# Four edits to a four-layer graph network on one core: group sums, mask pieces, the last tiles' transposes, and the place of a layer's columns

## The chip, the cores and the metric

The kernel runs on one core of a Trainium2 chip. A core has five engines with a queue of their own each: TensorE (PE, matrix products; its weight loads are listed as PEld), VectorE (DVE), ScalarE (ACT), GpSimd (POOL) and SyncE (SP, which only issues DMAs here). SBUF is the working memory of 128 partitions, PSUM holds the results of PE in 8 banks per partition, and HBM is the main memory. Sixteen DMA engines move data between HBM and SBUF. The metric is the device time of one execution in microseconds; lower is better.

## The reference

Four layers run one after the other over 3327 nodes with 512 features and one adjacency matrix `adj` of 3327 x 3327. Each layer's result is added to its input and normalised by rows. Layers 0, 2 and 3 are attention over neighbours with 8, 8 and 4 heads; layer 1 takes the mean of the first 64 neighbours.

```python
def attention(h, adj, W, a):             # layers 0, 2 and 3
    Wh = h @ W                           # split into heads
    e = leaky_relu((Wh @ a1)[:, None] + (Wh @ a2)[None, :], 0.2)
    p = softmax(where(adj > 0, e, -9e15), axis=neighbours)
    return p @ Wh                        # per head; layers 2 and 3 put elu on it

def mean_layer(X, A):                    # layer 1
    keep = (A > 0) & (cumsum(A > 0, axis=1) <= 64)
    nb_mean = (keep @ X) / max(keep.sum(axis=1), 1)
    xj = leaky_relu(nb_mean @ W_nb.T + b_nb)
    return leaky_relu(X @ W_line.T + b_line) + where(keep.sum(axis=1) > 0, xj, 0)

x = layernorm(x + attention_0(x)); x = layernorm(x + mean_layer(x))
x = layernorm(x + attention_2(x)); x = layernorm(x + attention_3(x))
```

## The kernel before

The nodes are padded to 3328, that is 26 tiles of 128 (`NT`), in two halves of 13 tiles or 1664 columns (`HALF`, `IW`). A half is cut for PE into four column ranges of 448, 448, 384 and 384 (`CUTS`); the first two together are `WA` = 896 columns, the last two `WB` = 768.

**Attention of layers 0 and 2** (`unit8`, L659, called by `attention8`). Eight units run in order. Units 0 and 7 take two heads and one half of the columns each; units 1 to 6 take one head and all 3328 columns ("wide"). The units form four groups: unit 0; units 1 to 3; units 4 to 6; unit 7. A unit has 26 steps, one for each tile `j` of neighbours:

- DVE makes `t` (L695) from the row values `rb` of the head, a column value and the mask: one operation of 128x3328, or two of 128x1664. There are three `t` buffers. Layer 0 reads the mask from the SBUF array `mask0`, layer 2 from the tiles `mk`.
- ACT makes `y` from it (L696), which is needed for the denominators.
- PE multiplies `t` with the values `vj` into `po` (L717, 16 matmuls), then adds the denominators of the step before into two PSUM banks `pd` (L675: the function `den`). The first half of the columns lies in rows 0 to 63 of `pd` and fills 448 columns of each bank, the second in rows 64 to 127 and fills 384.

A job may be hung to each step: one from the list `background`, then one from the list `aside`. At the end of a unit ACT copies `po` to `ob` (L732); four transposes by PE and four stores of `hd` follow as background jobs of the next unit.

At the end of a group the denominators are read. ACT copies `pd` to `db` in four copies, two of 64x448 (L771) and two of 64x384 (L772). A background job `sums` on step 2 of the next unit multiplies them down with PE into `pe` (L780); the job `reciprocals` on step 4 makes `rec` of them with six DVE operations (L788 to L790). The last group takes another way.

**The mask of layer 0.** Its first half is made before the attention begins. The second half is made during units 0 and 1, as `aside` jobs: `mask_steps` (L873) yields a list of steps; step k has SP load piece k of the adjacency matrix into a buffer `raw`, and sets the mask from piece k - lag, on DVE (L870) or, for 4 of 9 pieces, on ACT (L869). A piece has 416 columns, so there are 104; three buffers, a lag of 2, and three steps hung to each step of the unit. From step 13 of unit 1 on PE counts the columns of that half of the mask (`count_jobs`, L889, matmuls at L900).

**Layer 1** (`sage`, L949) accumulates each of the 26 tiles with 52 matmuls (L1139). `output` (L1114) turns the sum into the tile `y`, stores it, and for all tiles but the last loads it again by four DMAs in blocks of 32x32 as `yx`. `job1` makes the transposed tile `xT` in `project1` (L259): by a DVE transpose from `yx` (L263), or from `y` with four PE transposes and an ACT copy (L267, L268). `job2` makes the projection for layer 2 from it (L277). Both are hung to steps of the next tiles' accumulation: `job1` of tile 24 at step 21 of tile 25, its `job2` behind it.

**Layer 3** (`third`, L1173) first finishes layer 2 tile by tile and projects each tile with the weights `wsb`, which POOL loads (L144), then runs an attention of its own. The arrays `sden` and `sm` are made in `piece_columns` (L251), where POOL sets them to zero; they lie in the pool `col3` with the layer's other columns, below `wsb` in memory. The space is that of layer 2's attention, whose pools start with a row buffer `rbb` (13,312 B per partition) and layer 2's own `sden`.

**What sets the order.** PE runs in the order in which the program is written (`manual_schedule`, L63). On the other engines a planner puts the instructions into an order ahead of time, by its own estimate of when each can start, the earlier written first among those that can; `keep_in_program_order` holds an instruction behind the one written before it on its engine. The engines then run that order strictly. The planner also derives every wait, those for memory that an earlier tile still uses among them.

Of the kernel before, what the change touches and what calls it, by code (L numbers as in the profile page):

```python
# [13 lines left out]
ALU = mybir.AluOpType  # L14
# [4 lines left out]
P = 128  # L19
# [13 lines left out]
def kernel(  # L33
# [10 lines left out]
    nc = tc.nc  # L44
    N, F = x.shape
    NT = (N + P - 1) // P
# [4 lines left out]
    HALF = NT // 2  # L51
    FW = F // 2
    assert F == 512 and NT % 2 == 0 and N < NP and NT < 32
    IW = HALF * P
    NA = (HALF + 1) // 2
    WA, WB = NA * P, IW - NA * P
# [41 lines left out]
    c1 = const.tile([P, 2, 16], F32, name="c1")  # L98
# [6 lines left out]
    for e in range(2):  # L105
        nc.vector.tensor_tensor(c1w[:, :, e, :], c1[:, :, 8 * e:8 * e + 4], c1[:, :, 8 * e + 4:8 * e + 8],
                                op=ALU.add)
# [551 lines left out]
    def unit8(self, pools, n, ring, background, aside, ending=None):  # L659
        tp, yp, vp, sp, po_p = pools  # L660
        u = UNITS[n]
# [3 lines left out]
        if u.first:  # L665
            self.pd = [po_p.tile([P, 512], F32, name=f"pd{c}") for c in range(2)]
            self.seen = set()
        pd, seen = self.pd, self.seen
        f0 = u.h * D
        FV = D if u.wide else 2 * D  # L670
# [91 lines left out]
        def by_head(a, k):  # L762
            t0 = u.base(k) // P
            return a[:, t0:t0 + HALF, :].rearrange("p t (s k) -> p t k s", k=2)[:, :, u.section(k), slots]

        db = sp.tile([P, WA], F32, name="db", bufs=1)
        if WB < WA:
            nc.gpsimd.memset(db[64:, WB:], 0.0)
        if not end:
            for c in range(2):  # L770
                nc.scalar.copy(db[:64, c * (WA // 2):(c + 1) * (WA // 2)], pd[c][:64, :WA // 2])  # L771
                nc.scalar.copy(db[64:, c * (WB // 2):(c + 1) * (WB // 2)], pd[c][64:, :WB // 2])  # L772
            held = []

            def sums():
                pe = qp.tile([P, HALF, 2, 2 * NS], F32, name="pe", tag="q")
                held.append(pe)
                for q in range(HALF):
                    e = int(q >= NA)
                    nc.tensor.matmul(pe[:, q, :, :], db[:, (q - e * NA) * P:(q - e * NA + 1) * P],  # L780
                                     c1[:, :, 8 * e:8 * e + 8], start=True, stop=True)

            def reciprocals():
                pv = held[0].rearrange("p t o (k s) -> p t o k s", k=2)
                for k in range(2):
                    r_ = by_head(rec, k)
                    tc.keep_in_program_order(
                        nc.vector.tensor_tensor(r_, pv[:, :, 0, k, slots], by_head(self.rc, k), op=ALU.mult))  # L788
                    nc.vector.tensor_tensor(r_, pv[:, :, 1, k, slots], r_, op=ALU.add)
                    nc.vector.reciprocal(r_, r_)  # L790

            return jobs[:2] + [sums, nothing, reciprocals] + jobs[2:]

        for c in range(2):
            ins = nc.vector.transpose(db[:64, c * (WA // 2):(c + 1) * (WA // 2)], pd[c][:64, :WA // 2])
# [153 lines left out]
    def sage(first, first_pool, xin, prev, nxt, wsrc, dst, ring):  # L949
# [5 lines left out]
        with tc.tile_pool(name="sg_z", bufs=1, reuse_waits="tile") as zp, \  # L955
# [138 lines left out]
            with tc.tile_pool(name="sb_w", bufs=1, reuse_waits="tile") as wp, \  # L1094
                    tc.tile_pool(name="sb_k", bufs=1, reuse_waits="tile") as kpb, \
                    tc.tile_pool(name="sb", bufs=1, reuse_waits="tile") as sp, \
                    tc.tile_pool(name="sb_ps", bufs=1, space=PSUM, reuse_waits="tile") as ps, \
                    tc.tile_pool(name="sb_pk", bufs=1, space=PSUM, reuse_waits="tile") as pkp:
                pools_k.append(kpb)
                wsb = wp.tile([P, FC, 2, FW + nxt.H], F32, name="wsb")  # L1100
                load_wide(wsb, wsrc, nc.sync)

                def bank(e):
                    return qp.tile([P, 512], F32, name="pw1", tag="q") if e else \
                        ps.tile([P, 512], F32, name="pw0")

                bnb = wp.tile([P, F], F32, name="bnb")
                nc.gpsimd.dma_start(out=bnb, in_=bn.to_broadcast([P, F]))

                seed(pkp, None)  # L1110
                carry_in(FIRST)
                carry_in(FIRST + 1)

                def output(acc, t):  # L1114
                    xi = sp.tile([P, F], F32, name="xi")
                    nc.gpsimd.dma_start(out=xi, in_=xid[t * P:(t + 1) * P, :])
                    y = sp.tile([P, F], F32, name="y", bufs=2)
                    nc.vector.scalar_tensor_tensor(y, acc, cnt[:, 1, t:t + 1], bnb, op0=ALU.mult, op1=ALU.add)
                    nc.vector.scalar_tensor_tensor(y, y, 0.01, y, op0=ALU.mult, op1=ALU.max)
                    nc.vector.scalar_tensor_tensor(y, y, cnt[:, 2, t:t + 1], xi, op0=ALU.mult, op1=ALU.add)  # L1120
                    norm_rows(sp, [y], t)
                    store_tile(dst, y, t, nc.sync)
                    if t == NT - 1:
                        return y

                    yx = sp.tile([P, FC, P], F32, name="yx")
                    for q in range(4):
                        nc.sync.dma_start(out=yx[32 * q:32 * q + 32].rearrange("p c (g f) -> p c g f", g=4),
                                          in_=dst[t * P:(t + 1) * P, :].rearrange("(g a) (c q f) -> q a c g f", g=4, q=4, f=32)[q])
                    return yx  # L1130

                jobs, side = [], []
                for b in range(len(blocks)):
                    t0, i0 = blocks[b]
                    for s in range(G):
                        acc = ps.tile([P, F], F32, name="acc", bufs=2)
                        for t in range(NT):
                            for c in range(2):
                                nc.tensor.matmul(acc, kts[b, t][:, s * P:(s + 1) * P], zs(t, c),  # L1139
                                                 start=t == 0 and c == 0, stop=t == NT - 1 and c == 1)  # L1140
                            if (s * NT + t) % 4 == 1:
                                kept()
                                carry_in(len(kts) // 2 + 1)

                            if jobs and (t == 9 and t0 + s > 1 or t == 21):
                                jobs.pop(0)()
                            if side and t == 14:
                                side.pop(0)()
                        if t0 + s == 0:
                            tc.keep_in_program_order(nc.vector.tensor_copy(  # L1150
                                wsb[:, :, :, FW:], wa[nxt.li].rearrange("p c (e h) -> p c e h", e=2)))
                        y = output(acc, t0 + s)
                        held = {}

                        def job1(y=y, t=t0 + s, held=held):
                            held["xT"] = nxt.project1(sp, ps, y, t, t < NT - 1)

                        def job2(t=t0 + s, held=held):
                            nxt.project2(sp, bank, wsb, held["xT"], t)
                            if t == HALF - 1:  # L1160
                                side.extend(nxt.prepare_steps(sp, 0, "xT", 1))

                        jobs += [job1, job2]
                    if b == len(blocks) - 2:
                        for j in range(mask_tiles.FIRST):
                            mask_tiles.load(j, 0, nc.gpsimd)
                        nxt.first_rows = nxt.wide_rows(ring, UNITS[0])
                while jobs:
                    jobs.pop(0)()
                nxt.mean(sp, bank, wsb)  # L1170


    def third(first):  # L1173
        with tc.tile_pool(name="col3", bufs=1) as cp:
            rp = mask_tiles.early.tile([P, 2, IW], F32, name="rba")
            L3.columns(cp)
            L3.more_columns(cp)
            L3.piece_columns(cp)
            with tc.tile_pool(name="p_w", bufs=1, reuse_waits="tile") as wp, \
                    tc.tile_pool(name="p", bufs=3, reuse_waits="tile") as pp, \  # L1180
                    tc.tile_pool(name="p_f", bufs=2, reuse_waits="tile") as fp, \
# [50 lines left out]
            with tc.tile_pool(name="f3", bufs=2) as fp, tc.tile_pool(name="f4", bufs=1) as gp:  # L1232
# [115 lines left out]
                for k, (q0, n, _, add1, add2) in enumerate(lasts):  # L1348
# [6 lines left out]
                    if k > 0:  # L1355
                        scale(*lasts[k - 1][:2])
                scale(*lasts[-1][:2])

    L0, L2, L3 = Layer(0, 8, False), Layer(2, 8, True), Layer(3, 4, True)

# [2 lines left out]
    with tc.tile_pool(name="mask0", bufs=1, reuse_waits="tile") as mp0, \  # L1363
# [84 lines left out]
            return []  # L1448


        pieces = [(t, q, IW // 4) for t in range(NT) for q in range(4, 8)]
        rest = ExitStack()
        rawp = rest.enter_context(tc.tile_pool(name="raw", bufs=3))
        ring.insert(0, (rest.enter_context(tc.tile_pool(name="at_s0", bufs=1, reuse_waits="tile")), "rbb"))
        msteps = mask_steps(rawp, pieces, 2, [k for k in range(len(pieces)) if k % 9 in (1, 3, 5, 7)], True)

        def some(n):
            for f in msteps[n:n + 3]:
                f()

        ends = []
        attention8(L0, ring, first_jobs, [lambda n=n: some(n) for n in range(0, len(msteps), 3)],
                     ending=lambda sp: ends.extend(finish(f0, x, L0, 0, 2, 2, nc.sync, None, sp)))
        rest.close()

# [75 lines left out]
```

## Time and profile before

| | us |
|---|---|
| median of 3 runs | 3266.63 |
| lowest and highest | 3264.71 and 3269.53 |
| profiled execution | 3265.22 |
| its span, from the first instruction to the last | 3263.5 |
| attention of layer 0, last `ob` copies of units 0 and 7 | 255.3 and 958.2 |
| last accumulation of layer 1 ends | 1604.3 |
| attention of layer 2, last `ob` copies of units 0 and 7 | 1746.3 and 2421.1 |

The costliest rows of the profile's table of groups that the text below uses (busy time and mean of one; behind the second bar the idle time just before them and what ended most of it):

```profile
L695 DVE SCALAR_TENSOR_TENSOR t<-rba,qc,mask 128x3328 f32<-128x3328 f32 x78 | 281.9, 3679 | 8.3 <-PE po L717 8.0
L870 DVE TENSOR_SCALAR mask<-raw 128x832 fp8e4<-128x832 int32 x50 | 30.2, 614 | 25.4 <-DMA raw<-in_adjT_dram 25.4
L870 DVE TENSOR_SCALAR mask<-raw 128x416 fp8e4<-128x416 int32 x43 | 15.4, 371 | 7.3 <-DMA raw<-in_adjT_dram 7.1
L771 ACT COPY db<-pd 64x448 f32<-64x448 f32 x12 | 6.3, 527 | 0.1
L772 ACT COPY db<-pd 64x384 f32<-64x384 f32 x12 | 5.7, 474 | 0.1
```

A row names the line of the kernel, the engine, the operation, the tile written and those read, the shapes and the number of instructions. The 832-column rows are those of the mask's first half, which is made before the attention.

### The profile page before, as it was taken

How to read it: one execution, taken by the hardware profiler on the slowest of the kernel's cores; microseconds unless marked ns; L12 is line 12 of the kernel's file. 1: busy time of each engine (PE TensorE's matmuls, PEld its weight loads, DVE VectorE, ACT ScalarE, POOL GpSimd, SP SyncE). 2: the span in 40 equal slices, each digit the busy share in tenths (PEclk: the TensorE clock that was granted, in tenths of full speed). 3: DMA queues.
4: the chain of work that ended last, by engine and by line, in shares of the span. 5: the costliest groups of instructions: out<-in, count | busy, mean ns of one | idle time of the engine just before them, and what ended most of it. 6: DMA issues, size and time to landing. Idle time of an engine off the chain costs nothing. (4 is left out here: it accounts for less than half of the span.)

```text
span 3263.5 us, 46836 instructions
## 1 busy us (share of the span) xinstructions
PE 3161.3 (97%) x18738; PEld 1598.6 (49%) x18738; DVE 2624.2 (80%) x2328; ACT 2299.9 (70%) x1859; POOL 235.4 (7%) x384
## 2 busy tenths in 40 slices
PE   8999999999999999999899999999998999999997
PEld 7643343333434467777634333333447654455443
DVE  5799999999977645555499999999988666677886
ACT  2598888899873334444388998899987555558976
POOL 3100000000010011111100000000011000010110
PEclk9999999999999999999999999999999999999998
DMA  9554114111134345555331111011137211122311
GB/s 364 179 171 139 42 53 153 40 42 41 29 105 124 101 132 136 142 131 152 97 124 55 41 35 39 20 42 41 32 113 237 80 42 43 42 52 88 94 39 50
DMA packets 364212, 300.47 MB, mean 92 GB/s; under 512 B 235394, under 2 KB 304456, under 8 KB 362459
## 3 DMA queue, kind: packets, MB, share of 16 engines
q1 hardware_dynamic: 331803, 186.19, 19.9%
q0 software_dynamic: 26672, 103.60, 10.3%
q10 hardware_dynamic: 5520, 7.69, 0.7%
q8 instruction: 148, 2.42, 0.3%
q14 instruction: 69, 0.57, 0.1%
HBM read 220.53 MB, written 76.84 MB: 91 GB/s over the span
## 5 line engine op out<-in xcount | busy, mean ns | idle before, releaser
L696 ACT ACTIVATE y<-t,bi,sc 128x3328 fp8e4<-128x3328 f32 (+1 forms) x520 | 1342.7, 2604 | 144.6 <-PE pd L675 91.2
L717 PE MATMUL po<-t,vj 128*64 128x448 f32 (+1 forms) x6656 | 1266.6, 522 | 15.4 <-DVE t L695 14.3
L717 PEld LDWEIGHTS po<-t,vj 128*64 128x64 f32 x6656 | 450.4, 137 | 699.4 <-issue 621.2
L451 PE MATMUL po<-t,vj 128*128 128x448 f32 (+1 forms) x1664 | 607.2, 518 | 1.4 <-DVE t L428 1.4
L428 DVE SCALAR_TENSOR_TENSOR t<-rba,qc,mk 128x1664 f32<-128x1664 f32 x208 | 404.1, 1949 | 163.8 <-PE po L451 145.9
L431 ACT ACTIVATE y<-t,bi,sc 128x1664 fp8e4<-128x1664 f32 x208 | 358.4, 1767 | 198.1 <-PE pd L403 190.3
L451 PEld LDWEIGHTS po<-t,vj 128*128 128x128 f32 x1664 | 307.8, 190 | 272.7 <-issue 181.0
L695 DVE SCALAR_TENSOR_TENSOR t<-rba,qc,mk 128x3328 f32<-128x3328 f32 (+1 forms) x130 | 379.8, 2987 | 11.2 <-DMA mk<-md 7.5
L695 DVE SCALAR_TENSOR_TENSOR t<-rba,qc,mask 128x3328 f32<-128x3328 f32 (+1 forms) x130 | 381.8, 2986 | 8.3 <-PE po L717 8.0
L695 DVE SCALAR_TENSOR_TENSOR t<-rbb,qc,mask 128x3328 f32<-128x3328 f32 (+1 forms) x130 | 381.5, 2985 | 6.6 <-PE po L717 4.1
L695 DVE SCALAR_TENSOR_TENSOR t<-rbb,qc,mk 128x3328 f32<-128x3328 f32 (+1 forms) x130 | 379.9, 2985 | 5.7 <-PE po L717 4.9
L1139 PE MATMUL acc<-zs,kt 128*128 128x512 f32 x1352 | 359.9, 420 | 0.0
L277 PE MATMUL pw<-wsb,xT 128*128 128x264 f32 (+1 forms) x1248 | 305.0, 400 | 17.7 <-ACT xT L268 5.1
L1139 PEld LDWEIGHTS acc<-zs,kt 128*128 128x128 f32 x1352 | 255.7, 189 | 52.2 <-PE pk L990 0.8
L277 PEld LDWEIGHTS pw<-wsb,xT 128*128 128x128 f32 x1248 | 243.5, 199 | 62.7 <-ACT xT L268 10.0
L997 ACT CAST pk<-cy 128x512 f32<-128x512 bf16 x169 | 99.1, 587 | 222.9 <-DVE kt L1011 216.4
L675 PE MATMUL pd<-y,sden 128*32 128x448 fp8e4 (+1 forms) x3328 | 241.3, 343 | 0.0
L1011 DVE SCALAR_TENSOR_TENSOR kt<-pk,mb 128x512 fp32r<-128x512 f32 x169 | 115.4, 684 | 116.6 <-PE pk L1008 115.4
L675 PEld LDWEIGHTS <-sden 128*32 128x32 bf16 x3328 | 86.7, 96 | 139.2 <-issue 119.6
L283 DVE TENSOR_TENSOR vt<-pw,dc 128x256 f32<-128x256 f32 x156 | 58.6, 417 | 96.5 <-ACT dc L278 90.5
L1037 PE MATMUL pz<-wn,xT 128*128 128x512 f32 x208 | 96.2, 606 | 6.2 <-DMA wn<-in_wnT_dram 5.9
L967 POOL DMA_DIRECT2D cy<-ctd x91 | 68.1, 748 | 366.3 <-ACT pk L997 297.1
(213 smaller groups left out, 2119.9 us busy)
## 6 DMA issues: line engine op xcount, KB each, us to landing
vj<-v SPq DMA_DIRECT2D x156, 128.0 KB
cy<-ctd POOLq DMA_DIRECT2D x78, 256.0 KB, 4.3
raw<-in_adjT_dram SPq DMA_DIRECT2D x42, 416.0 KB
h<-hd SPq DMA_DIRECT2D x61, 256.0 KB
raw<-in_adjT_dram SPq DMA_DIRECT2D x75, 208.0 KB
v<-vt SPq DMA_DIRECT2D x50, 256.0 KB
xr<-x POOLq DMA_DIRECT2D x45, 256.0 KB, 3.4
md<-mask SPq DMA_DIRECT2D x26, 416.0 KB
```

The source lines that it names most:

```text
L277: nc.tensor.matmul(pw[e][:, :FW + H], xT[:, c, :], wsb[:, c, e, :], start=c == 0, stop=c == FC - 1)
L428: nc.vector.scalar_tensor_tensor(t, rb[k], self.qc[:, j, h:h + 1], mask_at[0](j, i0, IW), op0=ALU.max, op1=ALU.mult)
L431: nc.scalar.activation(y, t, AF.Sigmoid, bias=self.bi[:, j, h:h + 1], scale=self.sc[:, j, h:h + 1], saturate=False)
L451: nc.tensor.matmul(po[c][k * D:(k + 1) * D, :z - a_], vj[:, j % 2, k * D:(k + 1) * D], ts[k][:, a_:z], start=j == 0, stop=j == NT - 1)
L675: nc.tensor.matmul(pd[c][32 * kk:32 * kk + 32, :w_], lhsT, rhs, start=(kk, c) not in seen, stop=last and j == NT - 1)
L695: nc.vector.scalar_tensor_tensor(to, ro, self.qc[:, j, h:h + 1], m, op0=ALU.max, op1=ALU.mult)
L696: nc.scalar.activation(yo, to, AF.Sigmoid, bias=self.bi[:, j, h:h + 1], scale=self.sc[:, j, h:h + 1], saturate=False)
L717: nc.tensor.matmul(po[c][k * D:(k + 1) * D, :z - a_], vj[:, j % 2, x_:x_ + D], t[:, k, a_:z], start=j == 0, stop=j == NT - 1)
L997: nc.scalar.copy(pks[k % 2], carry[b, t // 4 * 4][:, t % 4:t % 4 + 2, :])
L1011: nc.vector.scalar_tensor_tensor(kt, pk, NEIGHBOURS, mb[:, t:t + 2, :], op0=ALU.is_le, op1=ALU.mult)
L1037: nc.tensor.matmul(pz, xT[:, c, :], wn[:, c, :], start=c == 0, stop=c == FC - 1)
L1139: nc.tensor.matmul(acc, kts[b, t][:, s * P:(s + 1) * P], zs(t, c), start=t == 0 and c == 0, stop=t == NT - 1 and c == 1)
```

## The change

It has four parts.

1. **Group sums.** `pd` is copied in two copies of 128x448 instead of four. So that the 64 columns that the lower rows do not fill hold zeros, DVE sets them to zero when a group begins (groups 0, 1 and 2). POOL's zeroing of a part of `db` goes, but for the last group. `reciprocals` works on both heads or halves at once, in three DVE operations instead of six, and runs on step 6 of the unit instead of step 4; the first transpose job moves from step 5 to step 3.
2. **Mask pieces** of the second half have 832 columns instead of 416: 52 instead of 104, with two buffers instead of three and a lag of 1 instead of 2. A step of the unit takes one or two of them, four in three steps, so that they reach to step 13 of unit 1 instead of step 9.
3. **Layer 1's last two tiles**, not only the last, are transposed by PE.
4. **Layer 3's `sden` and `sm`** lie in a pool of their own at the other end of the memory.

```diff
@@ unit8
         if u.first:
             self.pd = [po_p.tile([P, 512], F32, name=f"pd{c}") for c in range(2)]
             self.seen = set()
+            if not u.half and WB < WA:
+                for c in range(2):
+                    nc.vector.memset(self.pd[c][64:, WB // 2:WA // 2], 0.0)
...
-        if WB < WA:
+        if end and WB < WA:
             nc.gpsimd.memset(db[64:, WB:], 0.0)
         if not end:
             for c in range(2):
-                nc.scalar.copy(db[:64, c * (WA // 2):(c + 1) * (WA // 2)], pd[c][:64, :WA // 2])
-                nc.scalar.copy(db[64:, c * (WB // 2):(c + 1) * (WB // 2)], pd[c][64:, :WB // 2])
+                nc.scalar.copy(db[:, c * (WA // 2):(c + 1) * (WA // 2)], pd[c][:, :WA // 2])
...
                 for q in range(HALF):
                     e = int(q >= NA)
-                    nc.tensor.matmul(pe[:, q, :, :], db[:, (q - e * NA) * P:(q - e * NA + 1) * P],
-                                     c1[:, :, 8 * e:8 * e + 8], start=True, stop=True)
+                    nb = WB // 2 // P
+                    x_ = q * P if not e else (q - NA) // nb * (WA // 2) + (q - NA) % nb * P
+                    nc.tensor.matmul(pe[:, q, :, :], db[:, x_:x_ + P], c1[:, :, 8 * e:8 * e + 8], start=True, stop=True)
 
             def reciprocals():
-                pv = held[0].rearrange("p t o (k s) -> p t o k s", k=2)
-                for k in range(2):
-                    r_ = by_head(rec, k)
-                    tc.keep_in_program_order(
-                        nc.vector.tensor_tensor(r_, pv[:, :, 0, k, slots], by_head(self.rc, k), op=ALU.mult))
-                    nc.vector.tensor_tensor(r_, pv[:, :, 1, k, slots], r_, op=ALU.add)
-                    nc.vector.reciprocal(r_, r_)
-
-            return jobs[:2] + [sums, nothing, reciprocals] + jobs[2:]
+                pv = held[0].rearrange("p t o (k s) -> p k t o s", k=2)
+
+                def both(a):
+                    if u.wide:
+                        return a.rearrange("p (k t) (s e) -> p k t s e", k=2, e=2)[:, :, :, slots, u.parity]
+                    return a[:, u.half * HALF:(u.half + 1) * HALF].rearrange("p t (s k) -> p k t s", k=2)[:, :, :, slots]
+
+                r_ = both(rec)
+                tc.keep_in_program_order(
+                    nc.vector.tensor_tensor(r_, pv[:, :, :, 0, slots], both(self.rc), op=ALU.mult))
+                nc.vector.tensor_tensor(r_, pv[:, :, :, 1, slots], r_, op=ALU.add)
+                nc.vector.reciprocal(r_, r_)
+
+            return jobs[:2] + [sums] + jobs[2:4] + [nothing, reciprocals] + jobs[4:]
@@ sage
-                    if t == NT - 1:
+                    if t >= NT - 2:
                         return y
...
-                            held["xT"] = nxt.project1(sp, ps, y, t, t < NT - 1)
+                            held["xT"] = nxt.project1(sp, ps, y, t, t < NT - 2)
@@ third
-            L3.piece_columns(cp)
+            sums = ExitStack()
+            L3.piece_columns(sums.enter_context(tc.tile_pool(name="more3", bufs=1, side="right")))
...
+                sums.close()
@@ layer 0
-        pieces = [(t, q, IW // 4) for t in range(NT) for q in range(4, 8)]
+        pieces = [(t, q, IW // 2) for t in range(NT) for q in range(2, 4)]
         rest = ExitStack()
-        rawp = rest.enter_context(tc.tile_pool(name="raw", bufs=3))
+        rawp = rest.enter_context(tc.tile_pool(name="raw", bufs=2))
...
-        msteps = mask_steps(rawp, pieces, 2, [k for k in range(len(pieces)) if k % 9 in (1, 3, 5, 7)], True)
+        msteps = mask_steps(rawp, pieces, 1, [k for k in range(len(pieces)) if k % 9 in (1, 3, 5, 7)], True)
 
         def some(n):
-            for f in msteps[n:n + 3]:
+            for f in msteps[4 * n // 3:4 * (n + 1) // 3]:
                 f()
...
-        attention8(L0, ring, first_jobs, [lambda n=n: some(n) for n in range(0, len(msteps), 3)],
+        attention8(L0, ring, first_jobs, [lambda n=n: some(n) for n in range(len(msteps) * 3 // 4 + 1)],
```

## The prediction

> **What bounds the kernel now.** I read the page's busy table first, then TensorE's gaps in time, then for each gap the timeline of the engine it waited for.
>
> ```profile
> PE 3161.3 (97%) x18738; PEld 1598.6 (49%) x18738; DVE 2624.2 (80%) x2328; ACT 2299.9 (70%) x1859; POOL 235.4 (7%) x384
> ```
>
> PE is busy for 97% of the span, so an edit pays only where PE stands idle, or runs slowly after standing idle. Such places are few, and the four parts of the change lie at some of them. Between two ends of `ob` copies in the attention of layers 0 and 2, a unit that starts no group lasts some 94.5 us and PE is busy through all of it (unit 2 of layer 2: 94.5 of 94.5, windows of the trace), DVE for 93.8. What DVE or ACT saves there is worth nothing; what makes PE wait is lost in full.
>
> The timeline of DVE where unit 0 of layer 0 ends (start, duration, instruction; in brackets the idle time ahead and what ended it):
>
> ```profile
> 250.77 3.68 DVE L695 SCALAR_TENSOR_TENSOR t<-rbb,qc,mask 128x3328 f32<-128x3328 f32 x1
> 254.37 0.37 DVE L870 TENSOR_SCALAR mask<-raw 128x415 fp8e4<-128x415 int32 x1
> 259.01 0.38 DVE L870 TENSOR_SCALAR mask<-raw 128x416 fp8e4<-128x416 int32 x1 [4.27 <-DMA raw<-in_adjT_dram]
> 259.30 3.68 DVE L695 SCALAR_TENSOR_TENSOR t<-rbb,qc,mask 128x3328 f32<-128x3328 f32 x1
> ```
>
> DVE waits 4.27 us for a mask piece, in order, with the next product behind it; PE then starts 3.18 us late at 263.04. From 246 to 314 us PE loses 1.67 + 3.18 + 0.68 + 0.26 + 0.31 + 0.87 + 0.12 + 0.38 = 7.47 us to DVE (my list of PE gaps over 0.1 us).
>
> PE at the end of layer 1:
>
> ```profile
> 1596.53 7.81 PE L1139 MATMUL acc<-zs,kt 128*128 128x512 f32 x32
> 1607.41 6.83 PE L277 MATMUL pw<-wsb,xT 128*128 128x264 f32 x16 [3.07 <-DVE xT L263]
> 1614.77 0.66 PE L267 MATMUL pt<-ident,y 128*128 128x128 f32 x4 [0.53 <-ACT y L162]
> ```
>
> Tile 24's `xT` is late: its DVE transpose stood behind three operations of tile 25. The 16 matmuls after the gap take 6.83 us; the same 16 at 1593.16 took 3.72.
>
> POOL, then PE, at the start of layer 3:
>
> ```profile
> 2414.25 2.01 POOL L254 MEMSET sden<- 128x2288 bf16 x1 [42.69 <-DVE t L695]
> 2420.64 0.54 POOL L127 DMA_DIRECT2D xr<-x  x1 [3.17 <-ACT h L162]
> 2422.23 1.52 POOL L144 DMA_DIRECT2D wsb<-in_w_dram  x2
> ```
>
> ```profile
> 2429.00 0.89 PE L277 MATMUL pw<-wsb,xT 128*128 128x260 f32 x2 [4.02 <-DMA wsb<-in_w_dram]
> ```
>
> The weights are issued at 2422.23, and PE waits 4.02 us for them. From 2420 to 2440 the 16 DMA engines are 0.73 to 1.07 busy, before 2420 at most 0.15 (windows).
>
> ACT, then PE, where unit 1 of layer 2 begins:
>
> ```profile
> 1749.72 0.52 ACT L771 COPY db<-pd 64x448 f32<-64x448 f32 x1
> ...
> 1751.30 0.47 ACT L772 COPY db<-pd 64x384 f32<-64x384 f32 x1
> ```
>
> ```profile
> 1751.38 0.81 PE L675 MATMUL pd<-mk,sm 128*32 128x448 fp8e4 x8
> ```
>
> The copies end just as the next group's first sums in the same `pd` start.
>
> **What the Trainium skill says.** "DMA: Bandwidth & Descriptors", "Queues, rings and completion order": a DMA engine takes turns between queues packet by packet. The trace agrees: at 250.87 POOL issues the rows of unit 2, whose packets are 13,312 B and take 498 ns; a mask packet (1,664 B) takes 69. The piece issued at 250.88 needs 6.4 us to its last packet, the median of 100 pieces is 2.3. "TensorE: Matmul & The Clock Gate", part 1: after an idle window of about 3.4 us PE drops to half clock. The trace agrees (6.83 against 3.72 us, after a shorter gap of 3.07; clock 0.50 in 2430 to 2435). "PSUM — Partial Sum Buffer", "PSUM bank collisions raise a hardware error": different engines must be kept apart by bank and quadrant, not by address. So I take it that the new memset is ordered against copies and sums of its bank; no trace here shows it yet.
>
> **Group sums: +2.5 us.** Each of six group ends has two 64-row copies less: ACT 2 x (526 + 474) becomes 2 x 526 ns, 0.95 us saved, off the path. The divisions become 3 DVE operations from 6: by the rows (117 and 160, 172 and 195, 232 and 393 ns for 13 and 39 columns) I extend to 26 or 78 columns: about 0.4 us saved a group, 2.4 in all. The 12 new DVE memsets of 64x64 take it back: an estimate of 0.15 us each from the smallest DVE rows, 1.8. The later read gains nothing: DVE waited 0.5 us in all for `pe`. The POOL memset that goes held up only row loads whose buffers were not free. What counts is the new chain copies, memset, first sums. DVE is strictly in order and its slots are one product apart, 3.61 us in unit 1 of layer 2: 1749.07, then 1752.68. With half the copies done at 1750.8, the memsets fall at 1752.7, end at 1753.0, and PE waits 1.6 us. In the groups at 565 and 2032 us copies end at 566.9 and 2034.0, slots at 568.2 and 2035.3 precede the sums (570.6, 2037.6): nothing. At 255 us I take 0.9 of a possible wait of 1, since DVE's slot 266.8 follows the 265.98 of the sums. Bounds: 0, where the planner always finds an earlier slot, and +8.5 where each misses one (3 x 1.6 + 3.7).
>
> **Mask pieces: -5.5 us.** A set of 416 columns takes 371 ns (0.28 from start to start), of 832 columns 614: I take 0.53. The 5 of 9 pieces on DVE: 58 x 0.28 = 16.2 becomes 29 x 0.53 = 15.4. Four thirds of a piece per step instead of three small ones move work out of unit 0: there 43 x 0.28 = 12.1 becomes 19 x 0.53 = 10.1, so DVE reaches unit 1 about 2 us earlier, plus its small waits for pieces in unit 0 (0.34 + 0.37 + 1.08 + 0.13 + 0.22 + 0.09 = 2.2 us) where they vanish, with three `t` buffers as lead. In unit 1 a step costs DVE 3.60 + 0.39 = 3.99 for 14 steps instead of 4.07 for 10. Two pieces in flight hold 1,664 columns instead of 1,248, 1.5 steps instead of one, and beside the row load a piece of the same 128 packets brings twice the columns. SP issues half as many loads. I take 5.5 of the 7.47 us; bounds 0 (the stall at 255 merely moves) and -7.5.
>
> **Tile 24 by PE: -3.5 us.** Its four transposes (0.66, the row above) go into tile 25's accumulation at step 21, near 1602.4; `y` is ready since 1595.7, ACT is idle, so `xT` is there by 1603.8. The accumulation ends at 1605.0 instead of 1604.34, the projection follows at once at full clock: 1608.7 instead of 1614.24. Tile 25 then waits for its own chain: three DVE operations 2.2, statistics 0.75, table and root 1.6, DVE 0.6, ACT 0.8: `y` at 1611.1, where it now ends at 1614.7. SP loses four reloads, DVE one transpose. From there all shifts by 3.5. Bounds -1.5, if ACT loads its exponential table ahead of the root (1.28 more), and -4.5.
>
> **Layer 3's columns: -4 us.** By the pool sizes in the code, `wsb` (8,320 B per partition) lay at bytes 8,320 to 16,640 of the space that layer 2's attention leaves, over the row buffer (13,312 B) and layer 2's `sden`, read until PE's last sums at 2421.4. With 6,240 B gone from below it, it lies in the row buffer alone, free at 2414.1 when DVE has read it last. So POOL can issue it there; the memset ahead of it moves away. One MB passes in the idle 2414 to 2420. That takes it out of the crowd: `h<-hd`, for which DVE waits 4.18 us until 2436.49, should land near 2432.5, and the chain of `h` that starts PE at 2440.95 with it. PE's own waits for `wsb` (4.02 + 0.54 us) lie beside that chain and are not added. The memset waits under the other stack's `hb` and `red` until their stores land, estimate 2428 to 2431 from the 2425.26 issue of `dd`; behind it stand loads of `xr` that are used after 2454. Bounds -5.5, and 0 if POOL's order stays.
>
> **Sum.** +2.5 - 5.5 - 3.5 - 4 = -10.5. The profiled execution took 3265.22 (span 3263.5 and 1.7 around it), which gives 3254.7; the median of the runs is 1.4 above it: 3256 us.
>
> **Rivals.** (1) Partial: the piece in flight is caught by the row load anyway, or `wsb` is issued where it was. Without the mask gain -5.0, 3261.6; without layer 3's -6.5, 3260.1. For it: the row load is unchanged. Against it: more columns in flight. (2) The other side, slower: PE counts mask columns at step 13 of unit 1 in fixed order (L900, 317.49), and the piece before that is now planned for step 12, formerly 9. Sets run behind their steps: the last one, of step 9, ran after the product of step 13, at 313.75. If they still lag four to five steps, PE waits 3.7 us for each step beyond two: 4 such steps give +15 - 10.5 = +4.5, 3271. It decides from a lag of five steps on. Against it: 43,264 columns took 174 us with three small buffers; two large ones, at 2.8 + 2 to 3 us a turn (estimate: median 2.3, plus 0.5 for the bytes, plus a slot), are about a tenth faster. (3) The memset misses its slot everywhere: +6, so -4.5, 3262. (4) POOL's moved memset is put ahead of `wsb`: issue near 2431 + 2.8, PE 9 us later: about +3 in all, 3269.
>
> **How the numbers follow.** Less than 0.2% (6.5 us) cannot be told from no change. My forecast has 0.48, rival 1 0.24, 2 0.12, 3 0.10, 4 0.06. Faster takes the forecast and half of rival 1: 0.60; slower, half of 2, part of 4 and what I have not thought of: 0.12; same the rest, 0.28. Bounds summed give 3249 below (all at their best, -17.5) and 3272 above; I close at 3270. The forecast alone: 3249 to 3260.
>
> **What would show it.** Right: no PE gap of 3 us near 260; 16 projection matmuls in 3.7 us after layer 1's last accumulation; `wsb` issued by POOL near 2415, none of PE's 4 us. Wrong: PE waiting for DVE's `pd` memset by more than 2 us at 255, 565, 1744 and 2030; L900 in unit 1 waiting for a mask set; the POOL memset ahead of the weights.

## The result and the profile after

The changed kernel took 3257.87 us (median of 11 runs, 3252.65 to 3261.62), the kernel before beside it 3264.71 us. The ratio is 0.9976, with 95% interval 0.9967 to 0.9986: 7.8 us faster, between 4.6 and 10.8. A second series beside other kernels gave 0.9979 (0.9972 to 0.9986). The profiled execution took 3255.54 us with a span of 3253.8, 9.7 us less than the one of before. The time forecast was 3256, from a sum of -10.5 us on the profiled execution of before; the measured interval holds a gain of that size.

The busy line of the page hardly moves, as it should: the work is the same, and only TensorE's idle time and clock can change.

```profile
PE 3160.6 (97%) x18742; PEld 1603.0 (49%) x18742; DVE 2622.6 (81%) x2292; ACT 2290.4 (70%) x1827; POOL 233.7 (7%) x378
```

To see where the time went I took instructions that stand in both traces in the same place of the program and compared their start times. The shift, after minus before, is +1.3 us ahead of layer 0's attention (the loads at the start vary by that much between executions), -1.3 after unit 1 of layer 0, -0.7 in layer 1, -3.2 after its end, -1.9 after unit 1 of layer 2, -8.6 from the first products of layer 3 on, and -8.8 at the last matmuls; the other 0.9 us of the span lie behind them. So the gain arises in layer 0, at the end of layer 1 and at the start of layer 3, and the start of unit 1 in layer 2 gives some back. Each is read below, with the lines that answer to those shown of before. Line numbers are those of each run's own kernel, so L698 here is L695 of before.

DVE where unit 0 of layer 0 ends:

```profile
249.78 0.60 DVE L878 TENSOR_SCALAR mask<-raw 128x831 fp8e4<-128x831 int32 x1
250.28 3.69 DVE L698 SCALAR_TENSOR_TENSOR t<-rbb,qc,mask 128x3328 f32<-128x3328 f32 x1
258.32 0.60 DVE L878 TENSOR_SCALAR mask<-raw 128x831 fp8e4<-128x831 int32 x1 [4.35 <-DMA raw<-in_adjT_dram]
258.83 7.27 DVE L698 SCALAR_TENSOR_TENSOR t<-rbb,qc,mask 128x3328 f32<-128x3328 f32 x2
```

```profile
262.56 4.71 PE L720 MATMUL po<-t,vj 128*64 128x448 f32 x16 [2.97 <-DVE t L698]
```

The wait for the mask piece that I expected to go is there, 4.35 us where it was 4.27, and PE's gap behind it is 2.97 us where it was 3.18. The row load is issued at 250.17 and this piece at 250.41. What layer 0 gains comes from smaller waits, which are read with the experiments.

PE at the end of layer 1:

```profile
1604.01 3.72 PE L277 MATMUL pw<-wsb,xT 128*128 128x264 f32 x16
1611.32 1.04 PE L267 MATMUL pt<-ident,y 128*128 128x128 f32 x4 [3.60 <-ACT rc L281]
1613.09 6.37 PE L277 MATMUL pw<-wsb,xT 128*128 128x264 f32 x16 [0.73 <-ACT xT L268]
```

Tile 24's projection follows without a gap, in 3.72 us. The idle time now stands ahead of tile 25, and tile 25's 16 matmuls are the slow ones.

POOL, then PE, at the start of layer 3:

```profile
2412.51 1.51 POOL L144 DMA_DIRECT2D wsb<-in_w_dram  x2 [41.75 <-DVE t L698]
2418.73 0.55 POOL L127 DMA_DIRECT2D h<-hd  x1 [4.71 <-ACT h L162]
...
2432.26 2.01 POOL L254 MEMSET sden<- 128x2288 bf16 x1 [8.80 <-DMA hd<-hb]
```

```profile
2423.26 7.66 PE L277 MATMUL pw<-wsb,xT 128*128 128x260 f32 x32 [0.24 <-ACT xT L268]
2435.21 1.97 PE L267 MATMUL pt<-ident,h 128*128 128x128 f32 x8 [4.29 <-ACT h L162]
2437.00 5.68 PE L277 MATMUL pw<-wsb,xT 128*128 128x260 f32 x16
2447.25 0.72 PE L267 MATMUL pt<-ident,h 128*128 128x128 f32 x4 [4.57 <-ACT h L162]
```

The weights are issued ahead of everything else, 9.7 us earlier than before, and the 4.02 us of PE are gone.

DVE, then PE, where unit 1 of layer 2 begins, the place that gives back:

```profile
1738.65 10.87 DVE L698 SCALAR_TENSOR_TENSOR t<-rbb,qc,mk 128x3328 f32<-128x3328 f32 x3
1749.53 0.19 DVE L670 MEMSET pd<- 64x64 f32 x2
```

```profile
1742.46 5.81 PE L720 MATMUL po<-t,vj 128*64 128x448 f32 x32 [1.01 <-ACT ob L735]
1749.70 0.56 PE L678 MATMUL pd<-mk,sm 128*32 128x448 fp8e4 x8 [1.43 <-DVE pd L670]
```

The two memsets take 0.19 us together, but they stand behind the third of three products in DVE's order, and PE waits 1.43 us for them.

### The profile page after: what moved, and what is told of

Its sections match the earlier page's. It is cut to its first block, busy times and chain, and to the rows that moved or that the text cites. A ratio compares the mean times of both kernels' runs of the same rounds, so it can differ in the third digit from the quotient of the medians.

```text
span 3253.8 us, 46658 instructions
## 1 busy us (share of the span) xinstructions
PE 3160.6 (97%) x18742; PEld 1603.0 (49%) x18742; DVE 2622.6 (81%) x2292; ACT 2290.4 (70%) x1827; POOL 233.7 (7%) x378
## 4 chain that ended last, share of the span: by engine, by line
PE 84%; DVE 6%; issue 4%; DMA 3%; ACT 2%; SPq 0%; POOL 0%; ACTq 0%; POOLq 0%; DVEq 0%
PE po L720 34%; PE po L451 16%; PE acc L1147 9%; PE pd L678 8%; PE pw L277 6%; DVE t L698 3%; PE pz L1045 3%; PE pi L1048 3%; DMA raw<-in_adjT_dram 2%; PE pd L403 2%; PE pk L1016 1%; PE pt L742 1%; PE pe L784 1%; PE pt L267 0%; DMA h<-hd 0%
## 5 line engine op out<-in xcount | busy, mean ns | idle before, releaser
L698 DVE SCALAR_TENSOR_TENSOR t<-rba,qc,mask 128x3328 f32<-128x3328 f32 (+1 forms) x130 | 380.7, 2986 | 11.1 <-PE po L720 11.0
L698 DVE SCALAR_TENSOR_TENSOR t<-rba,qc,mk 128x3328 f32<-128x3328 f32 (+1 forms) x130 | 379.6, 2985 | 10.9 <-PE pd L678 7.4
L698 DVE SCALAR_TENSOR_TENSOR t<-rbb,qc,mk 128x3328 f32<-128x3328 f32 (+1 forms) x130 | 379.7, 2984 | 6.9 <-PE po L720 6.4
L698 DVE SCALAR_TENSOR_TENSOR t<-rbb,qc,mask 128x3328 f32<-128x3328 f32 (+1 forms) x130 | 381.0, 2984 | 5.3 <-PE po L720 2.8
```

Source lines behind the costliest of these rows:

```text
L698: nc.vector.scalar_tensor_tensor(to, ro, self.qc[:, j, h:h + 1], m, op0=ALU.max, op1=ALU.mult)
```

## The experiments

All times are ratios to the kernel before, measured beside it; 0.001 is 3.27 us. Each kernel also left one profile, and lengths of stretches are taken between the same two instructions in each trace. Stretch S reaches from the first matmul to the end of unit 1 of layer 0, T from layer 1's last accumulation to the middle of unit 0 of layer 2, U from about there into unit 1, V from layer 2's last products to the end of layer 3's projections. PE's idle time in units 0 and 1 of layer 0 is the sum of its gaps over 0.1 us from the first product on. The kernels were measured in several series, each beside the kernel before; two kernels of different series are compared through their ratios. Group sums, mask pieces, tile 24 and layer 3's columns are the four parts.

| kernel | ratio (95% interval) | S us | T us | U us | V us |
|---|---|---|---|---|---|
| before | 1 | 359.5 | 90.6 | 79.0 | 143.9 |
| only group sums | 1.0020 (1.0013 to 1.0027) | 362.8 | 86.7 | 81.9 | 144.0 |
| only mask pieces | 1.0003 (0.9995 to 1.0011) | 364.2 | 90.4 | 79.0 | 143.9 |
| only tile 24 | 0.9993 (0.9985 to 1.0002) | 360.9 | 87.3 | 79.0 | 144.0 |
| only columns | 0.9972 (0.9960 to 0.9983) | 359.3 | 86.0 | 79.0 | 135.6 |
| tile 24 and columns | 0.9974 (0.9965 to 0.9983) | 361.1 | 86.9 | 80.7 | 137.3 |
| all but group sums | 0.9969 (0.9958 to 0.9981) | 363.2 | 87.0 | 79.0 | 137.8 |
| all but mask pieces | 0.9989 (0.9982 to 0.9995) | 363.3 | 88.3 | 81.9 | 137.2 |
| changed kernel | 0.9976 (0.9967 to 0.9986) | 358.4 | 88.1 | 80.2 | 137.3 |
| changed kernel again | 0.9979 (0.9972 to 0.9986) | 359.7 | 87.1 | 81.9 | 137.6 |
| `pd` cleared once a layer | 0.9969 (0.9957 to 0.9981) | 361.8 | 87.0 | 78.7 | 137.4 |
| row load late | 0.9965 (0.9952 to 0.9977) | 356.5 | 87.9 | 81.9 | 137.5 |
| second piece on VectorE | 0.9974 (0.9967 to 0.9981) | 359.2 | 88.4 | 80.2 | 137.5 |
| these three together | 0.9944 (0.9931 to 0.9958) | 354.1 | 87.1 | 78.7 | 137.9 |

**Each part alone.** Four kernels, each the kernel before with the lines of one part from the diff above; the group sums, for example, begin with

```diff
+            if not u.half and WB < WA:
+                for c in range(2):
+                    nc.vector.memset(self.pd[c][64:, WB // 2:WA // 2], 0.0)
```

Expected of the group sums: 

> Group sums alone, the other three parts as before. Prediction: +2.5 us. Reading of the two traces: PE waits about 1.4 us for the memset of pd at the start of unit 1 in layer 2 (1.25 us longer unit), and the first memset of layer 0 puts about 1.6 us in front of the first product there; the other starts cost nothing. So +1.3 to +3 us. Rival, that the shorter copies and fewer divisions pay for themselves: 0 or below.

Expected of the mask pieces: 

> Mask pieces of 832 columns alone. Prediction: -5.5 us, and no PE gap of 3 us near 260. Reading of the two traces: -2.5 to -4 us; the wait of 4.3 us for the piece that meets the row load at the end of unit 0 stays (PE gap of about 3 us near 260), only the short waits after it go. Rival, that the gain of the changed kernel in layer 0 comes from the group sums: about 0.

Expected of tile 24: 

> Tile 24 of the mean transposed by TensorE, alone. Prediction: -3.5 us. Reading of the two traces: the projection of tile 24 follows at once, tile 25 is 2.8 us earlier and 2.6 us of it are left when layer 2's attention is under way: -2.6 us.

Expected of the columns: 

> Layer 3's columns in a pool of their own, alone. Prediction: -4 us, from h landing 4 us earlier. Reading of the two traces: -6.6 us, of which about 4 are matmuls at full instead of half clock, since PE no longer stands idle for the weights. Rival, that part of it belongs to the other parts (the earlier end of layer 2): below 5 us.

Measured, as ratio times 3266: group sums +6.5 us (4.2 to 8.8), mask pieces +1.0 (-1.6 to +3.6), tile 24 -2.3 (-4.9 to +0.7), columns -9.1 (-13.1 to -5.6). The group sums are dearer than I had read from the traces; the columns came out higher, with 6.6 inside their interval; the mask pieces bring nothing alone, and tile 24's gain is not told from zero. With the mask pieces alone PE's gap near 260 stays, 3.05 us, as I had then expected. Their trace also shows a wait I had not looked at. ACT in that kernel as layer 0's attention starts:

```profile
138.67 1.28 ACT L869 ACT_TABLE_LOAD   x1 [4.00 <-DMA raw<-in_adjT_dram]
139.96 0.99 ACT L869 ACTIVATE mask<-raw,below 128x831 fp8e4<-128x831 int32 x1
140.86 10.09 ACT L696 ACTIVATE y<-t,bi,sc 128x1664 fp8e4<-128x1664 f32 x6
150.96 1.28 ACT L318 ACT_TABLE_LOAD   x1
```

and PE there (`rc` and `rr` are the row values that ScalarE prepares and copies for later units, `pr` their transposes; `ct` and `pn` belong to the count of the mask's columns):

```profile
152.60 1.04 PE L324 MATMUL pr<-ident,rc 128*8 128x128 f32 x8 [1.76 <-ACT rc L318]
156.15 1.23 PE L324 MATMUL pr<-ident,rc 128*8 128x128 f32 x5 [2.51 <-ACT rr L326]
```

The second piece goes to ACT, and stands in its order ahead of the first `y`. ACT waits 4.00 us for it; in the kernel before the first `y` starts at 135.30, with the small sets behind it. `rc` is then 4 us late and PE loses 1.76 + 2.51 us, where it lost 0.23 before. In exchange its three waits for `ct` (0.96 + 0.33 + 2.15) shrink to 0.26. In sum PE is idle about as long in units 0 and 1 as before, 14.5 against 15.2 us. That S is still 4.7 us longer in this trace goes with the clock: the matmuls of unit 1 take 5.0 us more, at a granted clock of 0.956 against 1.00. In the kernel without the group sums, which has the same pieces, that excess is 1.6 us, so much of it is this one execution.

**Two parts, and three parts.** The same diff with parts left out.

Tile 24 and columns: 

> Only tile 24's transposes and layer 3's columns, without group sums and mask pieces. If the parts add up as they measured alone (-2.3 and -9.1 us): ratio 0.9965, as fast as the changed kernel or faster, and the group sums and mask pieces together cost 3 to 4 us. If group sums and mask pieces help each other (the four parts alone add up to -3.9, the changed kernel has -7.8): 0.9976 or above. In layer 0 it should look like the kernel before: no wait of TensorE for pr, 3.4 us for ct.

All but the group sums: 

> The changed kernel without the group sums (the other three parts stay). Theory: the memset of pd costs 1.6 us ahead of layer 0's first product and 1.3 us at unit 1 of layer 2, so about 3 us faster than the changed kernel, ratio to before 0.9967 or below; no gap of PE behind the pd memset. Rival: the sums' shorter copies pay elsewhere, and the time stays at 0.9976.

All but the mask pieces: 

> The changed kernel without the mask pieces (three loads of 416 columns as before). Prediction: 5.5 us slower than the changed kernel, ratio 0.9993. Theory after the run of the mask pieces alone: nothing to 2 us slower, ratio 0.9976 to 0.9982, the waits of TensorE for ct come back (3.4 us in unit 0) and the waits for pr go (1.8 us).

Tile 24 and the columns alone are as fast as the changed kernel: -8.5 us (-11.4 to -5.6) against -7.8 and -6.9. So group sums and mask pieces together cost about 1 us, with an uncertainty of some 3.5, where I had forecast -3.0. Without the mask pieces the changed kernel has about half its gain (0.9989 against 0.9976 and 0.9979), though alone they bring none: the two seem to help each other, with intervals that still touch. Counted from tile 24 and the columns, the group sums cost 4.9 us without the pieces and 2.3 to 3.3 with them; the pieces gain 1.6 us without the sums and 3.3 to 4.2 with them. Each of these differences is uncertain by 3.5 to 5 us.

The stretch S says the same. With neither part it has 359.3 to 361.1 us in four traces, with the sums alone 362.8 and 363.3, with the pieces alone 364.2 and 363.2, with both 358.4 and 359.7. Much of it is waits that hide one another. The memset starts the first product 1.6 us later (PE's gap ahead of it is 2.53 us in place of 0.98), but the second product's wait falls from 2.76 to 1.97 and 2.29 us and the waits for `pr` from 4.27 to 1.77 and 3.06. PE's idle time in units 0 and 1 shows the whole: 13.9 to 15.7 us with neither part, 14.7 and 16.5 with the sums alone, 14.5 and 15.2 with the pieces alone, 10.0 and 11.9 with both. With the gap ahead of the first product, both parts together save some 4.6 us of idle time over the sum of what each does without the other, out of some 7.5 us by which S is shorter than that sum. The rest is not settled. Half clock differs between executions, and so does the time up to the first product, by 2.2 us among the kernels that do not clear `pd` there.

**`pd` cleared once a layer.** The tile `pd` is made at unit 0 and kept, and cleared once, behind the first four products:

```diff
+            if n == 0:
+                self.pd = [po_p.tile([P, 512], F32, name=f"pd{c}") for c in range(2)]
...
+            if n == 0 and j == 0 and WB < WA:
+                for c in range(2):
+                    tc.keep_in_program_order(nc.vector.memset(pd[c][64:, WB // 2:WA // 2], 0.0))
```

> The changed kernel with pd made once a layer: its 64x64 corners are cleared once, behind the first four products, not at each group's start. If the memset is what the group sums cost, PE's gap of 1.43 us at unit 1 of layer 2 goes and the first product of layer 0 comes 1.6 us earlier: 3 us faster than the changed kernel, ratio 0.9967. If the cost lies in the later read or the new order of jobs, the time stays.

DVE, then PE, where unit 1 of layer 2 begins:

```profile
1736.70 21.65 DVE L696 SCALAR_TENSOR_TENSOR t<-rbb,qc,mk 128x3328 f32<-128x3328 f32 x6
```

```profile
1744.11 5.81 PE L721 MATMUL po<-t,vj 128*64 128x448 f32 x32 [1.00 <-ACT ob L736]
1749.84 0.56 PE L676 MATMUL pd<-mk,sm 128*32 128x448 fp8e4 x8
```

DVE runs its products without a break and PE's 1.43 us are gone; the gap ahead of layer 0's first product is 0.97 us again. Both waits are the memset's, then. But in layer 0 nothing is won by it. PE there:

```profile
139.22 10.29 PE L721 MATMUL po<-t,vj 128*64 128x448 f32 x46 [2.76 <-DVE t L696]
152.98 1.04 PE L324 MATMUL pr<-ident,rc 128*8 128x128 f32 x8 [1.85 <-ACT rc L318]
156.53 1.23 PE L324 MATMUL pr<-ident,rc 128*8 128x128 f32 x5 [2.51 <-ACT rr L326]
```

The waits that the memset had hidden are back. PE is idle for 15.4 us in units 0 and 1 against 10.0 and 11.9 in the changed kernel's two traces, and S is 2.1 and 3.4 us longer. The ratio is 0.9969, as without the group sums at all, where PE's idle time is 15.2 us. The difference to the changed kernel has the expected size (2.3 to 3.3 us), but it is not shown: the intervals overlap, and of seven runs one at 3246.59 us carries it; their median is 3257.97 us against 3257.87 and 3257.46 for the changed kernel.

**Row load late.** The rows of unit 2 are loaded at step 15 of unit 1, behind a write of one column that holds the DMA back:

```diff
+            if n == 1 and self.li == 0 and j == 15:
+                r_ = ring.pop(0)
+                ring.append(r_)
+                r_ = r_[0].tile([P, 2, IW], F32, name=r_[1])
+                tc.keep_in_program_order(nc.vector.memset(r_[:, 0, :1], 0.0))
+                nc.gpsimd.dma_start(out=r_.rearrange("p k i -> p (k i)"),
+                                    in_=self.rd[UNITS[2].h:UNITS[2].h + 1, :].to_broadcast([P, NP]))
```

> The changed kernel, but the row load of unit 2 in layer 0 starts at step 15 of unit 1 (behind a write of one column, after the last mask piece) and not at the end of unit 0. If the row load is what holds the mask piece, DVE's wait of 4.35 us near 254 and PE's gap of 2.97 us near 260 go: about 3 us faster than the changed kernel, ratio 0.9967. Rival, that the piece is late because only two buffers are turned over: the wait stays.

DVE at the end of unit 0:

```profile
248.23 0.59 DVE L889 TENSOR_SCALAR mask<-raw 128x831 fp8e4<-128x831 int32 x1
248.73 3.67 DVE L701 SCALAR_TENSOR_TENSOR t<-rbb,qc,mask 128x3328 f32<-128x3328 f32 x1
252.32 0.58 DVE L889 TENSOR_SCALAR mask<-raw 128x831 fp8e4<-128x831 int32 x1
252.83 7.27 DVE L701 SCALAR_TENSOR_TENSOR t<-rbb,qc,mask 128x3328 f32<-128x3328 f32 x2
```

No wait is left there: it was the row load that held the piece, and not the number of buffers. In time it is -11.4 us (-15.7 to -7.5) against -7.8 and -6.9, from five runs; what it gains alone isn't told from zero. S is 1.9 and 3.2 us shorter than in the changed kernel's two traces. A later piece now comes 0.93 us late, and PE waits 1.13 us near 305, where the changed kernel had no wait.

**Second piece on VectorE.**

```diff
-        msteps = mask_steps(rawp, pieces, 1, [k for k in range(len(pieces)) if k % 9 in (1, 3, 5, 7)], True)
+        msteps = mask_steps(rawp, pieces, 1, [k for k in range(len(pieces)) if k % 9 in (1, 3, 5, 7) and k > 1], True)
```

> The changed kernel with the second mask piece set by VectorE, not by ScalarE. In the changed kernel ScalarE's first instruction in layer 0's attention is the set of that piece, for which it waits 4.3 us, with the first y behind it. Theory: that wait makes PE's waits for pr (4.3 us together in the run of the mask pieces alone). So y starts near 136 instead of 141.8, the waits for pr go, up to 4 us faster than the changed kernel, 2 if the waits for ct come back. Rival, that the chain over rc on VectorE sets it: the waits stay.

ACT as layer 0's attention starts:

```profile
133.64 1.28 ACT L699 ACT_TABLE_LOAD   x1
135.71 7.36 ACT L699 ACTIVATE y<-t,bi,sc 128x1664 fp8e4<-128x1664 f32 x4 [0.79 <-DVE t L698]
```

The first `y` starts at 135.71 in place of 141.76, and PE's waits for `pr` are 0.63 us in place of 1.77 and 3.06. The mechanism is as stated. The time is not: 0.9974, the changed kernel's within the interval. The second product's wait is back at 2.76 us, from 1.97 and 2.29. The waits for `ct` are 0.45 and 1.82 us here (0.29 and 1.83 in the repeated changed kernel), and the matmuls of unit 1 take 3.2 us longer than in the changed kernel's first trace, at a granted clock of 0.955 against 0.985, so that this profile cannot show the gain either.

**All three, and the changed kernel again.**

> The changed kernel with all three: pd cleared once a layer, the row load of unit 2 at step 15, the second mask piece on VectorE. If the three waits are the cost and don't hide one another: 3 + 3 + 2 to 4 us faster than the changed kernel, ratio 0.9950. If they hide one another: 0.9965, as each alone.

> The changed kernel again, beside the others: ratio 0.9976 as before (0.9967 to 0.9986). In its trace the waits of 1.4 us at unit 1 of layer 2 and of 3 us near 260 are found again; the stretches in which matmuls run at half clock lie elsewhere in layer 0 and 2, and with them the time of each stretch moves by up to 3 us.

The three together give 0.9944 (0.9931 to 0.9958), a median of 3246.76 us: 18.3 us faster than the kernel before, and some 11 faster than the changed kernel measured beside it, whose interval lies clear of this one. The forecast for gains that add up, 0.9950, lies in this interval; the one for waits that hide one another, 0.9965, does not. In its trace S is 4.3 and 5.6 us shorter than in the changed kernel's two, and U 1.5 and 3.2 us. Together the three edits are shown to gain, though against the changed kernel none alone is told from zero. The repeated changed kernel shows the same waits, and different half-clock stretches: the products of layer 2 from unit 1 to the last unit take 647.7 us in its trace and 644.5 in the first.

## Why the forecast held, step by step

The total was near by luck. The four parts alone measured +6.5, +1.0, -2.3 and -9.1 us, -3.9 in sum, where the forecast had +2.5, -5.5, -3.5 and -4; errors of both signs cancelled. The rest came with the parts being together, which the forecast did not consider; a sum of four runs is uncertain by some 6 us, so how much of it that is stays open. (A slip in its bounds: the upper, 3272, counts from the profiled execution and the lower from the median; from the median it would be 3273.6.) By its own steps:

**Mask pieces, -5.5: this step failed.** It took that a wait at the end of unit 0 would go because "two pieces in flight hold 1,664 columns instead of 1,248" and DVE would come earlier. The wait stayed at 4.35 us, since a piece issued beside the row load lands with it: DVE is released at 258.3, and the rows land at 258.1. The Trainium skill's "DMA: Bandwidth & Descriptors", "Queues, rings and completion order", which the forecast cited for the turns between queues, agrees: this piece needed 7.0 us to its last packet, and the usual piece of its kernel 2.9. I drew the wrong sum from it, for twice the columns in the same 128 packets do not bring a piece in sooner when its packets take turns with those of 13,312 bytes. The step also left out ScalarE: the second piece now heads ACT's order in layer 0. What it got right are the short waits in unit 1, 2.6 us before, of which none over 0.2 us is left in the changed kernel's two traces. It did not name PE's 3.4 us of waits for `ct` in unit 0, which also go (0.3 us at most is left), nor those for `pr`, which come. Alone the part measured +1.0 us, and beside the group sums it gained 3.3 to 4.2. Rival 1 had no gain from the pieces; its 3261.6 us did not come, because the columns gave more and the pieces did help beside the sums. Of rival 2, the counts waiting for a late piece, the traces show nothing; the last piece is set at 319.44, and PE's longest wait behind it is 1.71 us for `ct` at 332, where the kernel before had 1.11.

**Group sums, +2.5: right in kind, too small.** The wait of 1.6 us at unit 1 of layer 2 was measured at 1.43. The groups at 565 and 2032 us wait for nothing, as said; at 255 the changed kernel has no wait, and the one without mask pieces has 0.99. What the step did not price is the first memset of layer 0: in the changed kernel it waits 1.45 us for ACT to read a tile of the PSUM space that it takes over, with the first four products behind it.

```profile
133.66 0.27 DVE L335 SCALAR_TENSOR_TENSOR bi<-qc,sc 128x104 f32<-128x104 f32 x1
135.38 0.19 DVE L670 MEMSET pd<- 64x64 f32 x2 [1.45 <-ACT ms L301]
135.47 7.46 DVE L698 SCALAR_TENSOR_TENSOR t<-rba,qc,mask 128x1664 f32<-128x1664 f32 x4
```

Nor did it price the clock. Without a memset there, the stretch U is 78.7 to 79.0 us in seven traces and 80.7 in one; with it, 80.2 in two and 81.9 in four. The extra 1.7 us are products at half clock behind the group sums. They come in one of eight traces without the memset and in four of six with it, so it is not shown that the memset brings them. Alone the part measured +6.5 us.

**Tile 24, -3.5: mechanism right, size probably too large.** The forecast put the transposes of tile 25 at 1611.1; they start at 1611.32, in a kernel that is 0.6 us early there, so 2.8 us of the 3.5 were won up to that point. "From there all shifts by 3.5" did not hold. Its base, 6.83 us for 16 matmuls at half clock, was one outcome of two: behind the same wait of 3.07 us the other three kernels without this part need 3.80, 6.67 and 3.80 us. The first of them, the group sums alone:

```profile
1611.34 3.80 PE L277 MATMUL pw<-wsb,xT 128*128 128x264 f32 x16 [3.07 <-DVE xT L263]
```

The wait and the half clock moved to tile 25 (3.60 us, then 6.37). There the half clock came every time: behind this wait of 3.60 us, and one of 0.73 us after the transposes, the 16 matmuls take 5.24 to 6.67 us in all ten traces with the part. The stretch T has 86.0 to 90.6 us in four traces without the part, mean 88.4, and 86.9 to 88.4 in ten with it, mean 87.5. The runs of the part alone (-2.3 us, -4.9 to +0.7) rule out neither 3.5 nor nothing.

**Layer 3's columns, -4: right, too small.** `wsb` is issued at 2412.5 (I said near 2415), the POOL memset at 2432.3, after the loads that matter, so rival 4 is out; DVE's wait for `h` is 0.71 us in place of 4.18. The mis-sized term is "PE's own waits for `wsb` lie beside that chain and are not added". As idle time they do. But the matmuls behind such a wait ran at half clock. The stretch V is 143.9 to 144.0 us in four traces without the part and 135.6 to 137.9 in ten with it; in the first pair 6.6 us shorter. PE's gaps in it add up to 18.75 us before and 16.11 after. So 2.6 us of the 6.6 are idle time, and the other 4.0 us are matmuls that run faster: the granted clock in V is 0.91 before and 0.94 after. That is an account of one pair of traces and not an experiment on the clock. It fits the order of ACT's instructions before: its `rc` at 2450.22 waits for the slow matmuls of 2444.02, and the `h` that starts PE again at 2455.36 stands behind it.

## What to carry to other kernels

Where TensorE is 97% busy, price an idle gap at more than its length: the matmuls behind it may run at half clock, and whether they do differs between executions, so take a stage's time from several traces. A short write that clears a tile costs its place in an in-order queue, not its 0.1 us; ask what it waits for and what stands behind it. Try the parts of a bundled change alone and left out: here one part of four gained alone as much as all four together, and two others together paid nothing that could be measured. A wait that is removed may only uncover the next one, so look for its time at the end of the stage and not at its place.

## What the hardware showed beyond that

The Trainium skill's "TensorE: Matmul & The Clock Gate", part 1, says that the window in which activity is counted runs free and does not start with the kernel, so that the moment at which the clock changes depends on where in it the first matmul falls. The four outcomes behind one wait of 3.07 us, two slow and two fast, fit that. The forecast had quoted the page with an idle window of about 3.4 us; these traces show that a wait shorter than that can cost the clock too, and behind the one of 3.60 us, with 0.73 us more soon after, it did so ten times in ten. Not expected was half clock with no gap ahead. The group sums are 26 matmuls of 16 columns in about 3.1 us, back to back; in 14 traces of six such places each, the 16 matmuls of the next product hold at least six at half clock in 36 of 84 cases, 13 of 14 at the last group of layer 0, one of 14 at 2040 us. Of the 5352 other groups of 16 products in layers 0 and 2 with no gap in the 40 matmuls ahead, two are slow in that way. The changed kernel's two traces at 2330 us show both outcomes, first the first execution, then the second:

```profile
2326.28 3.08 PE L784 MATMUL pe<-c,db 128*128 128x16 f32 x26
2329.28 3.02 PE L720 MATMUL po<-t,vj 128*64 128x448 f32 x16
```

```profile
2326.55 3.48 PE L784 MATMUL pe<-c,db 128*128 128x16 f32 x26
2329.96 5.82 PE L720 MATMUL po<-t,vj 128*64 128x448 f32 x16
```

The same 16 matmuls take 3.02 and 5.82 us. So the group sums go with the half clock, though not every time. That narrow matmuls count as little activity would explain it; no run here varied their width, so it stays a guess.
